# Layer 0 of a four-layer convolution kernel laid out by row block and group, with sampling weights built along the free axis

## The chip, the cores and the metric

The kernel runs on one core of one Trainium2 chip. The metric is the device time of one execution in microseconds (us). Before the change three runs gave a median of 5566.41 us (5564.74 to 5567.42). The engines are named as in the profile: PE (matmul, with its weight loads PEld), DVE, ACT, POOL, and SP, which here only issues transfers.

## What is computed

An input x of shape (8, 128, 96, 96), float32, goes through four layers. Each adds to x a function of its normalised value (32 groups of 4 channels). Layer 0 is a deformable convolution; the change rewrites it:

```python
x = x + _L0_conv_ref(_gn(x), dw_w, dw_b, gn_w, gn_b, om_w, om_b)   # deformable, 8 groups x 9 taps
x = x + conv3x3(_gn(x), L1_kernel)                                 # dense, 128 -> 128
x = x + layer2(_gn(x))                                             # depthwise on sign(x) and on x
x = x + layer3(_gn(x))                                             # scan over rows, 9 taps

# inside layer 0
x1 = gelu(norm(depthwise3x3(x) + dw_b))            # norm over the whole image
om = einsum('nhwc,oc->nhwo', x1, om_w) + om_b      # per group: 18 offsets and 9 masks
samp = gather(y0, x0) * (1-ly)*(1-lx) + ...        # bilinear, at tap position + offset
out = sum over the 9 taps of samp * mask
```

Both kernels use that with small offsets (a flag is computed, and a slow branch with a table in DRAM is there for the rest) every sampled point lies within two rows and columns of its pixel. Bilinear sampling then is a sum over 25 shifts (sy, sx), -2 to 2 each, of a weight times the shifted image. The weight of a shift is a sum over taps of a product of two "tents" max(0, 1 - |offset - distance|), one in y and one in x, the first times the mask.

## The kernel before

**The planner.** In layers 0 to 2 work is written as tasks (`Plan.task`): engine, price, function, dependences, due time, buffers. When the kernel is built, `Plan.order` (from line 165) runs through time with these prices, starts on each free engine the ready task that is due first and for which buffers are free, and so gives each engine a fixed order. On the chip engines follow that order and wait on semaphores. A due time only sets this order; DMA issues on SP are tasks as well.

**Layer 0 before.** The partitions hold 64 channels of the upper and of the lower half of an image (NB = 2 halves); the other 64 channels lie in the free axis. Two padded images (`xqs`) are kept. An image is worked on in 12 bands of 2 x 4 rows, 96 bands in all, one per STEP = 25 of due time.

`image(i, at)` loads the rows (L499, L503), takes statistics on DVE (L563), normalises on ACT (L618), does the depthwise convolution in nine taps per band on PE (L654; three bands of the first image on DVE, L646 and L648), evicts (L674), squares for the statistics (L683) and stores x1 to DRAM (L691).

`chunk(i, c, at, made)` does a band: x1 is loaded (L757), gelu (L764), the offsets and masks are projected on PE (L774) into partitions that stand for (group, tap), evicted (L793), and made into three tents for y and three for x on ACT (L783, L806); L835 multiplies the y tents by the mask on DVE. POOL multiplies nine pairs of tents (L878). For each of the 25 shifts PE multiplies such a pair by a 0/1 matrix (L888), which sums over taps and spreads a group's weight over its channels, into PSUM; DVE multiplies by the shifted image (L905). The products are added in one of three ways, by a string written by hand (ADDERS): PE with an identity matrix into one bank pair (L865), POOL (L923), or DVE (L912). The residual is loaded (L847); ACT evicts the sum with its total (L932), squares it (L940), and SP stores y (L945). y_stats makes the statistics of layer 1 (L955 to L959).

**Layers 1 and 2.** `conv_chunk` loads ten rows of y (L1279), normalises (L1290), makes four combinations on POOL (L1297), multiplies on PE in 128x128 tiles (L1310) and sums on DVE (L1326, L1334, L1346). The layer-1 weights km1 are made during layer 0 (L527 to L540). Layer 2 follows in 64x64 tiles (L1423, L1430) and on DVE (L1444). Layer 3 is a scan over 96 rows (L1722).

Of the kernel before, what the change touches and what calls it, by code (L numbers as in the profile page):

```python
# [53 lines left out]
FIRST_ON_DVE = (3, 6, 9)  # L54
RES_ORDER = (1, 0, 2)


def shift_groups():

    places = list(enumerate(shift_places()))  # L60
    return [
        (ry, rx, [(n, s) for n, s in places if s[0] % NR == ry and s[1] % NR == rx])
        for ry in RES_ORDER
        for rx in RES_ORDER
    ]

ADDERS = ("PDPEPPEPEEPDEPEDEEPDEPPPD", "PEEPPDPEEPEDDPEEPEDPEPPED")  # L70
LAST_ADDERS = "EDPPEEEDPEPDPEEEDPEEDEPPE"

STEP = 25
OM_SLOT = 11.42
WT_AHEAD = 6.2
ADD_LAG = 1438957.19
DW_SLOT = 2.09
DW_PACE = 3.98  # L80
# [133 lines left out]
def kernel(  # L214
# [33 lines left out]
    NB, HC = 2, P // 2  # L248

    def half(j):  # L250
        return slice(j * HC, (j + 1) * HC)
# [43 lines left out]
    km1 = const.tile([P, 4, 3, P], F32, name="km1")  # L295
    ymv = const.tile([P, N, 2], F32, name="ymv")
    y1 = dram.tile([N, P, HW], F32, name="y1")
# [117 lines left out]
    places = shift_places()  # L415
    groups = shift_groups()
    HB = H // NB
    XR, XW = HB + 2 * RS, W + 2 * RS
    NST = HB // RB
    GR = GK // NB  # L420
    flag = const.tile([1, 1], I32, name="flag")
    with ExitStack() as ph:
# [3 lines left out]
        x1d = dram.tile([N, P, HW], F32, name="x1d")  # L426


        sel = wp.tile([P, len(places), HC], F32, name="sel")
        omq = wp.tile([P, NB, 3, P], F32, name="omq")  # L430
        omb = wp.tile([P, 3], F32, name="omb")
        shift = wp.tile([P, 2 * NR], F32, name="shift")
        for t in (sel, omq, omb, shift):
            nc.vector.memset(t[:], 0.0)
# [3 lines left out]
        gnbq = wp.tile([P, NB], F32, name="gnbq")  # L438
        for j in range(NB):
            rows = slice(j * HC, j * HC + GR)  # L440
            taps = slice(j * GR, (j + 1) * GR)
# [5 lines left out]
            put_off(shift[rows, :], c_shift[taps, :])  # L447
            put_off(omb[rows, :], om_b[:, taps].rearrange("k r -> r k"))
            for b in range(NB):
                for m in range(NB):  # L450
                    put_off(
                        omq[half(b), j, :, m * HC : m * HC + GR],
                        om_wT[half(j), :].rearrange("c (k r) -> c k r", k=3)[:, :, m * GR : (m + 1) * GR],
                    )
            put_off(sel[rows, :, :], c_sel[taps, :, half(j)])
# [4 lines left out]
        xqs = [wp.tile([P, XR, NB, XW], F32, name=f"xq{i}") for i in range(2)]  # L460

        def zero_edges(xq):
            nc.gpsimd.memset(xq[:, :RS, :, :], 0.0)
            nc.gpsimd.memset(xq[:, XR - RS :, :, :], 0.0)
            nc.gpsimd.memset(xq[:, RS : XR - RS, :, :RS], 0.0)
            nc.gpsimd.memset(xq[:, RS : XR - RS, :, RS + W :], 0.0)

        zero_edges(xqs[0])

        stage = xqs[1][:].rearrange("p r j w -> p (r j w)")[:, : NB * XR * W].rearrange("p (j r w) -> p j r w", j=NB, w=W)  # L470
        nmx = wp.tile([P, N], F32, name="nmx")
        ysum = wp.tile([P, N, 2, NST], F32, name="ysum")
        yd = wp.tile([P, N, 2], F32, name="yd")
        beyond = wp.tile([P, 2 * N * NST], F32, name="beyond")
        nc.vector.memset(beyond[:], 0.0)

        plan = Plan()
        for name, n, psum in (
# [4 lines left out]
            if psum:  # L483
                tiles = [pp.tile([P, CB, 512], F32, name=f"ps_{name}{k}") for k in range(n)]
            else:
                tiles = [wp.tile([P, NB, FB], F32, name=f"{name}_{k}") for k in range(n)]
# [1324 lines left out]
```

## Time and profile before

| what | us |
|---|---|
| median of three runs | 5566.41 |
| profiled execution, its span | 5563.9 |
| PE busy | 5382.1 (97%) |
| weight loads busy | 3019.0 (54%) |
| DVE busy | 4838.8 (87%) |
| ACT busy | 3375.6 (61%) |
| POOL busy | 4552.9 (82%) |
| first product of layer 0 starts (L905) | 121.3 |
| last matmul of layer 0 ends (L865) | 3439.8 |
| first matmul of layer 1 starts (L1310) | 3455.3 |
| layer 3 begins, about | 4800 |

The core's mean granted PE clock was 0.992. It moved 360.67 MB in 413,202 DMA packets; SP's queue had 386,080 of these. A group of the profile names the source line, engine, operation, output and inputs, shape and count, then busy time, mean ns of one, idle time of the engine just before, and what ended it. Busy time is a union: operations of one engine overlap at their ends, and records of matmuls overlap far more, so a mean duration is not a pitch. For a pitch the starts of successive instructions are compared in the timeline.

### The profile page before, as it was taken

To read this page: it belongs to the slowest core of one execution; us is meant where nothing else is said; L and a number is where in the kernel's file an instruction comes from. 1 tells how busy PE (TensorE), PEld (TensorE's weight loads), DVE (VectorE), ACT (ScalarE), POOL (GpSimd) and SP (SyncE) were. 2 spreads that over 40 slices of the span, in tenths; PEclk is the share of its full clock that TensorE was granted. 3 is DMA by queue.
4 is the path that set the end of the run, shared out by engine and by line. 5 is a ranking of instruction groups with operands and counts; after the bars stand their busy time and mean duration, and the time that the engine had idled before them with its cause. 6 is when DMAs were issued, how large, how long until landed. Compare 5 with 4: busy or idle time off the path is not lost. (4 is left out here: it accounts for less than half of the span.)

```text
span 5563.9 us, 128984 instructions
## 1 busy us (share of the span) xinstructions
PE 5382.1 (97%) x53121; PEld 3019.0 (54%) x53121; DVE 4838.8 (87%) x6858; ACT 3375.6 (61%) x4820; POOL 4552.9 (82%) x2834
## 2 busy tenths in 40 slices
PE   6999999999999999999999998999999999999999
PEld 3554454454454454454454444545455554699999
DVE  6889889889889889888888997699999998688887
ACT  5666756656756756656766663477787777533333
POOL 1999999999999999999999998699999998522222
PEclk9999999999999999999999999999999999999999
DMA  5122112122121221211111111222222222223232
GB/s 135 55 61 58 56 58 60 54 60 58 56 59 58 57 61 58 57 60 57 49 49 47 38 43 38 59 68 68 67 65 68 66 65 51 83 103 103 100 106 80
DMA packets 413202, 360.67 MB, mean 65 GB/s; under 512 B 239072, under 2 KB 410608, under 8 KB 412608
## 3 DMA queue, kind: packets, MB, share of 16 engines
q1 hardware_dynamic: 386080, 312.91, 20.0%
q10 hardware_dynamic: 26160, 37.86, 1.9%
q8 instruction: 423, 6.93, 0.5%
q0 software_dynamic: 368, 1.57, 0.1%
q14 instruction: 171, 1.40, 0.1%
HBM read 201.26 MB, written 150.99 MB: 63 GB/s over the span
## 5 line engine op out<-in xcount | busy, mean ns | idle before, releaser
L888 PE MATMUL ps_w<-wt,sel 64*64 64x384 f32 x19200 | 1856.5, 488 | 48.3 <-DVE h L835 15.1
L905 DVE TENSOR_TENSOR pr<-ps_w,xq 128x768 f32<-128x768 f32 x1824 | 1672.4, 950 | 203.0 <-PE ps_w L888 153.0
L878 POOL TENSOR_TENSOR wt<-h,h 128x768 f32<-128x768 f32 x864 | 1581.7, 1835 | 191.6 <-PE ps_w L888 112.5
L923 POOL TENSOR_TENSOR acc<-acc,pr 128x768 f32<-128x768 f32 x882 | 1615.6, 1833 | 64.3 <-DVE pr L905 49.9
L888 PEld LDWEIGHTS ps_w<-wt,sel 64*64 64x64 f32 x19200 | 748.0, 133 | 906.3 <-issue 279.7
L1310 PE MATMUL pv_C<-dC,km 128*128 128x384 f32 x2304 | 777.3, 492 | 11.2 <-POOL dC L1297 4.8
L865 PE MATMUL ps_s<-pr,idq 64*64 64x384 f32 x7536 | 759.5, 484 | 1.8 <-DVE pr L905 1.3
L1444 DVE SCALAR_TENSOR_TENSOR ps_C<-xqC,w2s,ps_C 128x768 f32<-128x768 f32 x674 | 684.9, 1016 | 84.2 <-ACT ps_C L1482 69.7
L793 ACT ACTIVATE o<-ps_w,omb 128x768 f32<-128x768 f32 x192 | 172.5, 898 | 807.3 <-PE ps_w L774 702.2
L1661 POOL TENSOR_TENSOR xtD<-xtD,cr 128x384 f32<-128x384 f32 x192 | 192.3, 1002 | 572.1 <-ACT cr L1660 509.8
L654 PE MATMUL ps_w<-xq,dwd 64*64 64x384 f32 x6696 | 635.5, 485 | 8.3 <-DVE h L835 3.4
L1310 PEld LDWEIGHTS pv_C<-dC,km 128*128 128x128 f32 x2304 | 426.6, 190 | 359.0 <-issue 49.6
L905 DVE TENSOR_TENSOR ps_w<-ps_w,xq 128x768 f32<-128x768 f32 x480 | 460.4, 959 | 97.2 <-PE ps_w L888 96.2
L783 ACT ACTIVATE h<-o,shift 128x768 f32<-128x768 f32 x576 | 533.1, 926 | 11.7 <-ACT o L793 0.8
L806 ACT ACTIVATE h<-h 128x768 f32<-128x768 f32 x576 | 485.9, 844 | 17.4
L1461 POOL TENSOR_TENSOR ptC<-ptC,ptC 128x768 f32<-128x768 f32 x255 | 472.8, 1854 | 1.1
L865 PEld LDWEIGHTS ps_s<-pr,idq 64*64 64x64 f32 x7536 | 309.4, 133 | 299.6 <-issue 159.2
L912 DVE TENSOR_TENSOR acc<-ps_w,acc 128x768 f32<-128x768 f32 x480 | 456.8, 952 | 6.8
L774 PE MATMUL ps_w<-x1c,omq 64*64 64x384 f32 x4608 | 436.3, 493 | 21.8 <-DVE pr L905 18.0
L654 PEld LDWEIGHTS ps_w<-xq,dwd 64*64 64x64 f32 x6696 | 284.4, 133 | 271.0 <-issue 119.7
L1722 PE MATMUL ps_b<-tr,km 128*128 128x192 f32 x2304 | 407.2, 325 | 2.8 <-DVE tr L1707 2.8
L1722 PE MATMUL ps_a<-tr,km 128*128 128x192 f32 x2304 | 405.5, 324 | 0.0
(201 smaller groups left out, 7162.3 us busy)
## 6 DMA issues: line engine op xcount, KB each, us to landing
ywC<-y SPq DMA_DIRECT2D x80, 480.0 KB, 3.9
acc<-in_x SPq DMA_DIRECT2D x192, 192.0 KB, 3.3
x1c<-x1d SPq DMA_DIRECT2D x192, 192.0 KB, 3.3
y<-y SPq DMA_DIRECT2D x96, 384.0 KB, 3.0
x<-oC SPq DMA_DIRECT2D x192, 192.0 KB, 2.8
out<-xtD ACTq DMA_DIRECT2D x24, 1536.0 KB, 5.7
x1d<-x SPq DMA_DIRECT2D x93, 384.0 KB, 2.8
xtD<-x SPq DMA_DIRECT2D x23, 1536.0 KB, 6.9
```

The costliest lines, as they stand in the source:

```text
L654: nc.tensor.matmul(ps.tile[half(j), b, :FB], dwd[half(b), j, t, :], xq[half(b), r0 : r0 + RB, j, c0 : c0 + W], start=(t == 0), stop=(t == ...
L783: nc.scalar.activation(h, o, AF.Abs, bias=shift[:, k * NR + r : k * NR + r + 1])
L806: lambda h=h: nc.scalar.activation(h.tile[:], h.tile[:], AF.Relu, bias=1.0, scale=-1.0),
L865: nc.tensor.matmul(total.tile[half(j), b, :FB], idq[half(b), :], pr.tile[half(b), j, :], start=first, stop=last)
L878: lambda wt=wt, hy=hy, hx=hx: nc.gpsimd.tensor_tensor(wt.tile[:], hy.tile[:], hx.tile[:], ALU.mult),
L888: nc.tensor.matmul(ps.tile[half(b), j, :FB], sel[half(j), n, :], wt.tile[half(j), b, :], start=True, stop=True)
L905: nc.vector.tensor_tensor(view(pr.tile), view(ps.tile), x_s, ALU.mult)
L923: lambda pr=pr, acc2=acc2: nc.gpsimd.tensor_tensor(acc2.tile[:], acc2.tile[:], pr.tile[:], ALU.add),
L1310: nc.tensor.matmul(flat(ps), km1[:, k, x_, :], d.tile[:, k, :, x_ : x_ + W], start=(x_ == 0), stop=(x_ == 2))
L1444: nc.vector.scalar_tensor_tensor(view, rows8(src, t), w[:, t : t + 1], view, ALU.mult, ALU.add)
L1461: lambda a=parts[0], b=pt: nc.gpsimd.tensor_tensor(a.tile[:], a.tile[:], b.tile[:], ALU.add),
L1722: nc.tensor.matmul(ps[:, at_f : at_f + nf], km[:, k, t, :], tr[:, par, :, v : v + HW2], start=(t == 0), stop=(t == NT - 1),)
```

## The change

The planner is kept. Layer 0 is written anew; layers 1 to 3 keep their work, apart from where layer 1 gets its weights and how it reads y.

- **Layout.** A chunk is one row out of every six: `BR = H // 16` = 6 chunks per image, 48 in all. Partitions are (row block y of 16, group g of 8); the free axis is (16 channels of the group, 96 columns). One padded image `xq` is kept in place of two, for the depthwise convolution.
- **Padded rows through DRAM.** After normalisation `copy_rows` stores the image, in padded rows of 100, to `xnd`; the shifted rows come back in the new layout, ten loads `xs` per image, five in use at a time. Border rows of zeros for `xnd` are stored at the start from ACT's queue.
- **Projection.** PE projects 2 x 108 rows of om for 1536 pixels in four tasks; ACT evicts, SP stores to `omd` and loads it back with (row block, group) in the partitions and taps in the free axis.
- **Weights.** ACT makes three tents for all taps in four passes and a fifth for the flag. POOL (DVE for the first chunk) makes the 25 weights of each (row block, group, column) in 18 operations along the free axis, with stride-zero operands; ACT copies them to PSUM, five shifts at a time.
- **Products.** DVE multiplies 128x1536: the weight is read from PSUM with stride zero over the 16 channels.
- **Sums.** PE adds each product with an identity in 16 tiles of 32x32 (row tile r to bank r, channel quarter f to output partitions 32 f). The residual is one more such add, by the standard deviation, of the middle row, so x is not loaded again; x's mean is added in layer 1's coefficients. No adds are left on DVE and POOL, and no selection by PE.
- **y** is stored by (row in block, row block, channel) in four transfers per chunk; layer 1 loads its ten rows in pieces that end at block borders. Its weights are loaded and made at the beginning of layer 1 (the same six operations). The branch with the table follows the new layout of y.

The diff's core:

```diff
-FIRST_ON_DVE = (3, 6, 9)
-RES_ORDER = (1, 0, 2)
...
-ADDERS = ("PDPEPPEPEEPDEPEDEEPDEPPPD", "PEEPPDPEEPEDDPEEPEDPEPPED")
-STEP = 25
+FIRST_ON_DVE = (2, 5, 8, 11)
+CH, SHIFT, PE_KEEP = 46.0, 9.0, 4.0
+LOAD_AT, NORM_AT, CONV_AT, CONV_STEP, CONV_PACE = -90, -45, -35, 18, 1.6
+OM_STEP, SLOT_AT, COPY_AT = 2.5, 25, -5
...
-    y1 = dram.tile([N, P, HW], F32, name="y1")
+    y1 = dram.tile([N, BR, YB, P, W], F32, name="y1")
...
+        omd = dram.tile([N * BR, YB, NG * GR, W], F32, name="omd")
+        xnd = dram.tile([N, BR, YB + 1, P, XW], F32, name="xnd")
...
+        for i in range(N):
+            for d, y in ((0, 0), (RS, YB)):
+                nc.scalar.dma_start(
+                    xnd[i, d : d + RS, y].rearrange("d c w -> c d w"), zero.rearrange("p (d w) -> p d w", w=XW)
+                )
...
+            ("s", 1, [P, NQ, 512], True, True), ("wb", 2, [P, 512], True, True), ("w", 1, [P, CB, 512], True, False),
+            ("xs", 5, [P, GC, XW], False, True), ("pr", 3, [P, GC, W], False, True), ("y", 1, [P, NQ, FB], False, True),
+            ("om", 1, [P, 3, K2, W], False, True), ("tt", 1, [P, 2, 3, K2, W], False, True),
+            ("wx", 2, [P, 3, 3, NS, W], False, True), ("x1", 2, [P, NB, FB], False, True),
+            ("x1c", 1, [P, YB, W], False, True), ("oe", 2, [P, YB, W], False, True),
...
+            def copy_rows(d):
+                r, up = (d - RS) % BR, int(d < RS)
+                for b in range(NB):
+                    for j in range(NB):
+                        nc.sync.dma_start(
+                            xnd[i, d, b * YB // NB + up : (b + 1) * YB // NB + up, half(j), :].rearrange("y c w -> c y w"),
+                            xq[half(b), RP + r : RP + HB : BR, j, :],
+                        )
...
+                        xnd[i, j % BR, j // BR : j // BR + YB].rearrange("y (g c) w -> (y g) (c w)", g=NG),
...
+                        omd[n, :, m * HM : (m + 1) * HM].rearrange("y r w -> r y w"), oe.tile[:HM]
...
+                    omd[n].rearrange("y (g k) w -> (y g) (k w)", g=NG),
...
+                (lambda: nc.scalar.activation(own(1), offs(), AF.Abs), [tt, om]),
+                (lambda: nc.scalar.activation(own(1), own(1), AF.Identity, bias=1.0, scale=-1.0), [tt]),
+                (lambda: nc.scalar.activation(own(0), offs(), AF.Relu, scale=-1.0), [tt, om]),
+                (lambda: nc.scalar.activation(own(2), offs(), AF.Relu), [tt, om]),
...
+                lambda: nc.scalar.activation(offs(), own(1), AF.Relu, scale=-1.0, accum_out=beyond[:, n : n + 1]),
...
+            on = nc.vector if n == 0 else nc.gpsimd
...
+                lambda: on.tensor_tensor(
+                    wx.tile[:, :, :, 1 : NS - 1].rearrange("p d y x w -> p d y (x w)"),
+                    tripled(rows(tx(1))),
+                    all_ty().rearrange("p d y x w -> p d y (x w)"),
+                    ALU.mult,
+                ),
...
+            def add_all(weights, of, first, last):
+                for r in range(NQ):
+                    for f in range(NF):
+                        rows32 = slice(32 * r, 32 * r + 32)
+                        nc.tensor.matmul(
+                            total.tile[32 * f : 32 * f + 32, r, :FB], weights(rows32, f), of(rows32, f), start=first, stop=last
+                        )
...
-                        nc.vector.tensor_tensor(view(pr.tile), view(ps.tile), x_s, ALU.mult)
+                        nc.vector.tensor_tensor(
+                            pr.tile[:],
+                            wb.tile[:, sx * W : (sx + 1) * W].unsqueeze(1).to_broadcast([P, GC, W]),
+                            slot.tile[:, :, sx : sx + W],
+                            ALU.mult,
+                        )
...
+                    to = y1[i, dy].rearrange("y p w -> (y p) w").rearrange("(r l f c) w -> f l r (c w)", r=NQ, l=32, f=NF)
+                    nc.sync.dma_start(to[f], y.tile[32 * f : 32 * f + 32])
...
+        def conv_weights(at):
...
+            ld = plan.task("SP", 0.6, lambda: nc.sync.dma_start(k3s[:], k1), [], at - 100, lag=4.0)
...
-                    y1[i, :, lo * W : hi * W].rearrange("p (r w) -> p r w", w=W),
...
+                r = lo
+                while r < hi:
+                    z = min(hi, (r // BR + 1) * BR)
+                    nc.sync.dma_start(
+                        yw.tile[:, top + r - lo : top + z - lo, 1 : W + 1],
+                        y1[i, r % BR : r % BR + z - r, r // BR].rearrange("d p w -> p d w"),
+                    )
+                    r = z
```

## The prediction

> **What bounds the kernel now.** I read the stages first (busy time by stretch), then the costliest groups, then single instructions in order of time for the true pitch of each operation. Stretches show us busy and, in brackets, instructions for PE, weight loads, DVE, ACT and POOL; then clock, DMA share and GB/s.
>
> ```profile
> 0.00:121.00 121.00, 69.49 (x740) 35.70 (x740) 76.96 (x182) 59.12 (x102) 4.54 (x14) 0.94 0.63 152
> 300.00:3100.00 2800.00, 2723.99 (x32808) 1320.70 (x32799) 2488.35 (x3000) 1765.49 (x2594) 2633.20 (x1471) 0.99 0.19 56
> 3100.00:3437.00 337.00, 335.41 (x4050) 147.57 (x4049) 332.04 (x378) 191.95 (x268) 323.27 (x181) 1.00 0.12 36
> 3437.00:3455.00 18.00, 4.15 (x32) 2.37 (x24) 2.86 (x17) 5.63 (x9) 4.53 (x23) 0.64 0.44 106
> 3455.00:4800.00 1345.00, 1324.31 (x8828) 671.57 (x8828) 1153.69 (x1758) 971.05 (x1090) 1226.62 (x863) 1.00 0.25 64
> ```
>
> Layer 0 is the first 3455 us of 5563.9: a 121 us start, 3316 us for 96 bands (414 us per image), an 18 us end. Layers 1-2 take 1345, layer 3 764; the change scarcely touches these.
>
> ```profile
> L888 PE MATMUL ps_w<-wt,sel 64*64 64x384 f32 x19200 | 1856.5, 488 | 48.3 <-DVE h L835 15.1
> L905 DVE TENSOR_TENSOR pr<-ps_w,xq 128x768 f32<-128x768 f32 x1824 | 1672.4, 950 | 203.0 <-PE ps_w L888 153.0
> L878 POOL TENSOR_TENSOR wt<-h,h 128x768 f32<-128x768 f32 x864 | 1581.7, 1835 | 191.6 <-PE ps_w L888 112.5
> L923 POOL TENSOR_TENSOR acc<-acc,pr 128x768 f32<-128x768 f32 x882 | 1615.6, 1833 | 64.3 <-DVE pr L905 49.9
> ```
>
> DVE and POOL idle mostly for PE's L888, and PE waits for almost nothing. The mean durations overlap, so I price by start to start:
>
> ```profile
> 3421.94 0.96 DVE L905 TENSOR_TENSOR ps_w<-ps_w,xq 128x768 f32<-128x768 f32 x1
> 3422.81 0.95 DVE L905 TENSOR_TENSOR pr<-ps_w,xq 128x768 f32<-128x768 f32 x1
> 3423.67 0.95 DVE L912 TENSOR_TENSOR acc<-ps_w,acc 128x768 f32<-128x768 f32 x1
> ```
>
> 768 elements cost DVE 0.87. L1346 (384) starts 0.47 before its successor, so each further 384 adds 0.40.
>
> ```profile
> 4005.01 0.82 PE L1423 MATMUL ps_C<-xqC,dgx 64*64 64x384 f32 x8
> 4005.76 8.03 PE L1310 MATMUL pv_C<-dC,km 128*128 128x384 f32 x24
> 4013.71 0.88 PE L1423 MATMUL ps_C<-vn,dgv 64*64 64x384 f32 x8
> ```
>
> A float32 matmul is two records; 24 follow each other in 8 us, 0.322 a round. In 64x64 tiles a round is four records starting some 7 ns apart, so eight cost 0.645. Changing between tile sizes adds 0.11 (last start to next start 0.41, against 0.30 between lines of one size).
>
> One image of before: PE 300 selects, 142 adds, 105 taps at 0.645 and 36 projections at 1.29: 399 of 414 us, 96%. POOL 218 x 1.77 = 386. DVE 360 x 0.87 + 36 x 0.93 + 24 x 0.47 + about 9 of small ones = 366. **PE bounds layer 0, POOL close behind.**
>
> **What the Trainium skill says.** "TensorE: Matmul & The Clock Gate", Part 3 (packing small matmuls): 16 tiles of 32x32 run together, measured at 660 ns as its span model gives, starts about 4 ns apart. The trace shows only four tiles of 64x64 doing this, 7 ns apart. "TensorEngine Tiling (Array Packing)", Key Properties: changing the mode drains the array; the trace's 0.11 agrees. "SBUF — State Buffer", Who interferes with whom: a DVE instruction with at most one SBUF input does not contend with GpSimd. L905 has one and keeps 0.87 beside a 94% busy POOL; the new product has one too. "DMA: Bandwidth & Descriptors", Specifications: below 512 B a transfer does read-modify-write. The trace's 384 B packets are nearly all reads from DRAM (mean 26 ns), its stores have 1536 B (78 ns), so no row shows small stores.
>
> **The change, part by part.**
>
> *Products.* 2400 of 768 elements become 1200 of 1536, at 0.87 + 0.80 = 1.67. The stride-zero operand in PSUM is not new: L1334 reads such a one.
>
> ```profile
> L1346 DVE TENSOR_TENSOR vn<-vn,pv_C 128x384 f32<-128x384 f32 x192 | 104.2, 549 | 14.3 <-PE pv_C L1310 14.3
> L1334 DVE TENSOR_TENSOR vn<-vn,pv_C 128x768 f32<-128x768 f32 x96 | 91.3, 951 | 25.6 <-PE pv_C L1310 25.2
> ```
>
> It takes 951, like L905's plain 950. So 150 x 1.67 = 250 per image. The 480 adds of L912 and 288 mask products of L835 leave DVE (85 per image). With bn_stats 11 and about 40 small ones of 0.2: **DVE 270 per image.**
>
> *PE.* All selections go. In their place are 26 adds per six-row chunk, each 16 tiles of 32x32. Unknown price: not below 0.645 (the stream is as long); not above 2.58 (four tiles at a time). Tiles alone argue for 0.645; sixteen starts of 7 ns (0.11) fit under a 0.322 round. I take 0.7. Projections 24 x 1.29 = 31, taps 108 x 0.645 = 70. In the instruction order PE changes tile size 880 times, 110 per image: 12. Sum 113 + 156 x 0.7 = 222; it ties with DVE only at 1.0.
>
> *POOL.* Its adds go; it builds the weights of 47 chunks, 18 operations of 15,744 elements together:
>
> ```profile
> L1297 POOL TENSOR_TENSOR dC<-ywC 128x392 f32<-128x392 f32 x384 | 357.7, 980 | 57.1 <-PE pv_C L1310 37.2 <-ACT ywC L1290 17.9 <-PE pv_C L1254 2.0
> L1400 POOL TENSOR_TENSOR sgC<-sgC,thC 128x960 f32<-128x960 f32 (+1 forms) x96 | 213.8, 2227 | 52.4 <-ACT thC L1395 52.3
> ```
>
> (2227 - 980) / 568 = 2.2 ns an element and 0.12 each: 37 us, against a DVE chunk of 45. There is one tt buffer: ACT's five 1728-element passes (8 us at L783's rate) must follow POOL's last read of it, of which the final 6 us of POOL work hide most. So about 40 per chunk. Stride-zero on POOL is not shown; below 37 has no reason, and it matters only above 45.
>
> *ACT.* About 26 us of a 45 us chunk: hidden, unless a weight copy to PSUM queues behind the 8 us of passes; I put that into the idle share below.
>
> *DMA and SP.* Per image: 12,300 small packets of x, 12,300 of x1 back, 20,700 of om out and 12,300 of padded rows out: 57,600 x 26 ns / 16 = 94 us. Then 25.6 MB in larger ones at 1536 B per 78 ns on 16 engines: 81. Together 175 of 280; if small stores cost double, 229. SP issues about 142 transfers x 0.6 = 85. Both fit.
>
> *Next image.* In PE's order its last tap stands at add 21 of chunk 3, so 2.2 chunks, 99 us, remain. What follows: coefficients 7, load 5, gelu 3, projection 10, om out 6 and back 6, passes 8, weights 37 = 82. It fits with 17 us to spare.
>
> *Start.* First product at 121.3 before. Added: weights of the first chunk on DVE (15,744 x 1.04 ns + 18 x 0.2 = 20), om through DRAM 12, behind five row loads 7, border zeros on ACT's queue (4,096 packets x 26 / 16 = 7), longer passes 5; less 6 for fewer coefficient steps and no selection: first product at 166.
>
> *End.* Last product to first layer-1 matmul: 18.6 before. A doubled eviction 0.7, three more stores 1.8, y loads in up to three pieces and the sum over places 2: 23. The layer-1 weights (six operations, 3 us) lie beside y's way through DRAM. The split y loads (1280 packets, 2 us more of landing) are hidden by three buffers and PE's 8 us per chunk. The branch with the table is not taken: nothing.
>
> *Sum.* 8 x 270 less 11 (first statistics lie in the start) = 2149 of DVE. The bounding engine reached 96% before; the same gives 2239. So 166 + 2239 + 23 = 2428 in place of 3455: -1027. With 3 for a slower first y load the span is 5563.9 - 1027 + 3 = 4540. The median of the runs stands 2.5 above the span: **4542 us.** At 99% and a start of 150 it is 4460, at 93% and 180 it is 4630.
>
> **Rivals.** (1) *Weights come late*: small stores cost double, the chain of 82 passes 99, DVE idles at each image's start. Against it: the spare 17; for it: one om, one tt, one projection buffer in PSUM. With 25 us per image: 4740. (2) *PE becomes the bound*: four streams from the same partitions run at half rate, 1.29 per add: (113 + 201) / 0.96 = 327 per image in place of 281: 4910. For it: the trace shows at most two streams. (3) *Slower than before*: the four column tiles of a row group take turns, 2.58 per add: 515 / 0.96 = 536 per image, about 6580. This decides from where an image takes (3455 - 166 - 23) / 8 = 408: add price (408 x 0.96 - 113) / 156 = 1.79. The two column tiles of L888 share a row group and don't take turns, which speaks against it. (4) Nothing gained, because the removed work was hidden: PE's 96% excludes most of that.
>
> **Numbers.** Forecast 0.74 (its own range 4450 to 4640), (1) 0.12, (2) 0.10, (3) 0.03, (4) 0.01. Range 4450 to 4740, which reaches into (1). About 0.2% (11 us) is what a measurement can tell. Faster 0.96, same 0.01, slower 0.03.
>
> **What would show it.** Products at 1536 elements starting 1.67 apart and DVE about 96% busy between 166 and 2405; adds near 0.7 start to start, PE near 80%; POOL near 85%. If PE is full and DVE waits for it, (2) holds; if DVE's gaps stand at every sixth chunk and end on POOL or DMA, (1). Wrong would be a product pitch above 1.8, or layers 1-2 longer by over 20 us.

## The result, and the profile after

The changed kernel takes **95,733.7 us** (median of four runs, 95,729.0 to 95,740.2), the kernel before 5565.84: 17.20 times as long, 95% interval 17.18 to 17.23. The prediction was 4542.

First the stretches of the changed kernel: us busy and, in brackets, instructions for PE, weight loads, DVE, ACT and POOL; then clock, DMA share and GB/s.

```profile
217.00:2793.00 2576.00, 2061.63 (x46675) 806.88 (x46671) 2161.04 (x1599) 1192.06 (x1570) 1722.10 (x845) 0.92 0.52 139
2793.00:93550.00 90757.00, 2595.64 (x6630) 1236.25 (x6598) 14075.08 (x21556) 294.38 (x327) 50211.88 (x55310) 0.51 0.11 19
93550.00:94843.00 1293.00, 1220.52 (x7436) 625.71 (x7436) 1148.76 (x1658) 868.31 (x968) 1128.34 (x818) 0.97 0.24 61
94843.00:95738.00 895.00, 870.83 (x6009) 806.05 (x6008) 713.64 (x1476) 365.01 (x701) 293.77 (x247) 0.99 0.28 93
```

The reader is to see that layer 0 in its new form is over at 2793, from the first product at 217 to the last, and that 90,757 us follow which are in no stretch of the kernel before. The costliest groups of the page say what runs there:

```profile
L1180 POOL DMA_INDIRECT gt<-table,idx x55296 | 50211.2, 908 | 40158.7 <-DVE wq L1176 22932.4
...
L1194 DVE TENSOR_REDUCE sm<-gt 96x128 f32<-96x4608 f32 x768 | 6011.9, 7828 | 26.5
...
L989 DVE TENSOR_TENSOR pr<-ps_wb,xs 128x1536 f32<-128x1536 f32 x1200 | 2016.3, 1746 | 396.9 <-PE ps_s L955 299.7
L955 PE MATMUL ps_s<-pr,idr 32*32 32x384 f32 x38400 | 1198.8, 517 | 239.2 <-DVE pr L989 231.8
```

L1180 and L1194 stand inside the branch with the table (L1084 to L1219). It works out layer 0 a second time, for offsets of any size: POOL issues 72 gathers for each of 768 rows, 55,296 in all, at 0.91 us each. The gathers keep POOL busy for 50,211 us of the branch; for 40,159 POOL idles before them, 22,932 of these waiting for DVE's L1176. The flag was set, so nearly all of the difference is a branch that the prediction took as not taken. (This branch reads the bias of the offsets anew, L1103, and so does not have the first of the faults below.) Three questions follow. Why is the flag set? What would the change have taken without that? And where is that off the prediction?

The products and sums are as foreseen. In the last image, which has no next image beside it, the timeline shows:

```profile
2759.15 33.36 DVE L989 TENSOR_TENSOR pr<-ps_wb,xs 128x1536 f32<-128x1536 f32 x20
...
2760.95 0.94 PE L955 MATMUL ps_s<-pr,idr 32*32 32x384 f32 x32 [0.73 <-DVE pr L989]
2762.61 0.94 PE L955 MATMUL ps_s<-pr,idr 32*32 32x384 f32 x32 [0.72 <-DVE pr L989]
```

Twenty products take 33.36 us, 1.67 each; PE waits 0.72 or 0.73 for each of them. In the trace 813 pairs of adds have no other matmul between them. Most of these adds wait for a product; the 350 that start less than 0.8 us after the one before start 0.67 after it (median), and none follows closer.

### The profile page after: what moved, and what is told of

The parts are those of the page before. It is cut to its first block, busy times and chain, and to the rows that moved or that the text cites. A ratio compares the mean times of both kernels' runs of the same rounds, so it can differ in the third digit from the quotient of the medians.

```text
span 95738.4 us, 299514 instructions
## 1 busy us (share of the span) xinstructions
PE 6846.6 (7%) x67518; PEld 3518.2 (4%) x67518; DVE 18194.9 (19%) x26516; ACT 2809.0 (3%) x3700; POOL 53364.9 (56%) x57227
## 5 line engine op out<-in xcount | busy, mean ns | idle before, releaser
L1180 POOL DMA_INDIRECT gt<-table,idx x55296 | 50211.2, 908 | 40158.7 <-DVE wq L1176 22932.4
L1187 DVE TENSOR_TENSOR gt<-gt,wq 96x4608 f32<-96x4608 f32 x768 | 3804.7, 4954 | 67801.5 <-DMA gt<-table,idx 67801.5
L1194 DVE TENSOR_REDUCE sm<-gt 96x128 f32<-96x4608 f32 x768 | 6011.9, 7828 | 26.5
L989 DVE TENSOR_TENSOR pr<-ps_wb,xs 128x1536 f32<-128x1536 f32 x1200 | 2016.3, 1746 | 396.9 <-PE ps_s L955 299.7
L955 PE MATMUL ps_s<-pr,idr 32*32 32x384 f32 x38400 | 1198.8, 517 | 239.2 <-DVE pr L989 231.8
L359 PE MATMUL ps_dw<-xn_g,dwd_g 128*128 128x384 f32 x3456 | 1139.7, 491 | 25.1 <-ACT xn_g L351 25.1
L1142 PE MATMUL om<-omw,xr 128*96 128x216 f32 x1536 | 772.2, 606 | 4263.4 <-DMA xr<-x1d 4250.3
L1177 DVE TENSOR_TENSOR wq<-wq,loc 96x72 f32<-96x72 f32 x3072 | 756.3, 288 | 0.0
L899 POOL TENSOR_TENSOR tt<-tt,om 128x2592 f32<-128x2592 f32 x47 | 267.5, 5692 | 851.1 <-ACT om L875 436.2
L359 PEld LDWEIGHTS ps_dw<-xn_g,dwd_g 128*128 128x128 f32 x3456 | 657.0, 190 | 503.6 <-ACT xn_g L351 25.8
L692 PE MATMUL ps_w<-xq,dwd 64*64 64x384 f32 x6336 | 593.2, 509 | 109.1 <-ACT x L721 100.5
L1791 POOL TENSOR_TENSOR xtD<-xtD,cr 128x384 f32<-128x384 f32 x192 | 192.1, 1001 | 573.0 <-ACT cr L1790 511.0
L955 PEld LDWEIGHTS ps_s<-pr,idr 32*32 32x32 f32 x38400 | 447.8, 106 | 925.8 <-DVE pr L989 618.7
```

The costliest lines, as they stand in the source:

```text
L359: nc.tensor.matmul(ps[:, b, :FB], dwd[:, t, :], xn[:, r0 : r0 + RB, c0 : c0 + W], start=(t == 0), stop=(t == K2 - 1),)
L692: nc.tensor.matmul(ps.tile[half(j), b, :FB], dwd[half(b), j, t, :], xq[half(b), r0 : r0 + RB, j, c0 : c0 + W], start=(t == 0), stop=(t == ...
L955: nc.tensor.matmul(total.tile[32 * f : 32 * f + 32, r, :FB], weights(rows32, f), of(rows32, f), start=first, stop=last)
L989: nc.vector.tensor_tensor(pr.tile[:], wb.tile[:, sx * W : (sx + 1) * W].unsqueeze(1).to_broadcast([P, GC, W]), slot.tile[:, :, sx : sx + W ...
L1142: nc.tensor.matmul(om[:W, 0, : 3 * GK], xr[:], omw[:], start=True, stop=True)
L1177: nc.vector.tensor_tensor(wq[:, :, q], wq[:, :, q], loc[:, 2, :], ALU.mult)
```

## Why the flag is set: two faults

These lines of the changed kernel matter and are not in the diff's core:

```python
        junk = wp.tile([P, NB, FB], F32, name="junk")                                  # L426
        bias_in, bias_by_g = (junk[0:1, j, : 3 * GK] for j in range(2))                # L427
...
                    bias_by_g.rearrange(...), bias_in.rearrange(...)                   # L517, DVE
                        b.tile[:HM, 0, m : m + 1], bias_by_g[:, ...], one[:], ...      # L540, PE
...
                        junk[:], x1.tile[:], AF.Square, bias=ndwb[:], accum_out=...    # L728, ACT
```

**Fault 1.** The bias of the offsets passes through the tile `junk`, into which L728 throws the squares of every band. The planner is not told that L540 must come first. The timeline of the changed kernel near the start:

```profile
53.60 0.25 DVE L517 COPY junk<-junk 1x216 f32<-1x216 f32 x1
61.60 0.92 ACT L728 ACTIVATE junk<-x,ndwb 128x768 f32<-128x768 f32 x1
...
66.08 0.51 PE L540 MATMUL ps_w<-one,junk 1*108 1x1 f32 x4 [0.88 <-DVE LyT L535]
```

PE reads at 66.08 as bias what ACT has written at 61.60: squares of a band. All offsets and masks get a wrong constant.

**Fault 2.** The check of the offsets (L875) reads 1 - |offset| from the tile `tt`, and the first weight operation (L899) multiplies the y tents in the same tile by the mask, in place. L899 depends on the tents alone (`chain = [tents]`), so the planner may put it first. The timeline of the second chunk:

```profile
207.66 1.63 ACT L868 ACTIVATE tt<-om 128x1728 f32<-128x1728 f32 x1
...
209.36 5.67 POOL L899 TENSOR_TENSOR tt<-tt,om 128x2592 f32<-128x2592 f32 x1 [207.54 <-ACT tt L868]
...
215.06 1.64 ACT L875 ACTIVATE om<-tt 128x1728 f32<-128x1728 f32 x1 [3.84 <-POOL tt L899]
```

The check starts when L899 has ended. In 17 of the 48 chunks of the trace it comes behind L899 like this, and a tent times a negative mask counts as an offset beyond 1. In those chunks ACT, which follows its planned order, also waits for POOL, 3.8 to 7.8 us each time and 93 together. (The expectations below have 18 chunks, 5.65 us and 102.)

I saw fault 2 first and took it for the whole cause (theory A, with theory B as its rival: another cause). Four runs tested this.

**e1: the check first.**

```diff
-            chain = [tents]
+            chain = [checks[-1:]]
```

> One dependence is added: the first weight operation of a chunk (L899) waits for that chunk's check of the offsets (L875). Theory A (18 of the 48 checks read the y tents after L899 has multiplied them by the mask, so the flag is set although no offset passes 1): the branch is not taken. The changed kernel's span less the branch (2799 to 93549 us) is 4988; the 18 waits of ACT for L899 (5.65 us each, 102 together) go too, of which some reaches the end: 4880 to 4990 us. Theory B (the flag is set for another reason: an offset really passes 1, or the column sums hold something else): about 95,700 us, as before the edit. The prediction on record would have 4542.

Measured: 95,536.0 us (95,527 to 95,540), ratio 17.18 (17.16 to 17.20). All 48 checks stood ahead of L899, and the branch was taken. Theory A as the only cause falls.

**e2: the flag times 0.**

```diff
-            nc.vector.tensor_scalar(flag[:], m2[:], 0.0, None, ALU.is_gt)
+            nc.vector.tensor_scalar(flag[:], m2[:], 0.0, None, ALU.mult)
```

> The order of the changed kernel is kept as it is, misplaced checks included; only the last step of the flag multiplies by 0 in place of comparing with 0, so the offsets no longer decide on the branch (that decision is left out). Theory A and theory B alike: the branch alone is the 90,000 us, so 4940 to 5000 us. If part of the time lay elsewhere (a slow path of layers 1 to 3, or waits in front of the branch), more than 5100. Against e1 it gives the price of the 18 waits of ACT alone: 0 if they are hidden, up to 102 us.

Measured: 4985.75 us (4973.4 to 4987.4), ratio 0.897 (0.895 to 0.898). The branch is the whole of the 90,000 us, and nothing else of that size is hidden in front of or behind it. This run leaves the decision out and keeps both faults, the wrong bias included, so it serves for timing alone.

**e3: the x half of the check alone.**

```diff
-                lambda: nc.scalar.activation(offs(), own(1), AF.Relu, scale=-1.0, accum_out=beyond[:, n : n + 1]),
+                lambda: nc.scalar.activation(
+                    om.tile[:, 0].rearrange("p k w -> p (k w)"), tt.tile[:, 0, 1].rearrange("p k w -> p (k w)"),
+                    AF.Relu, scale=-1.0, accum_out=beyond[:, n : n + 1],
+                ),
```

> The check reads and clears only the x half of the tents (864 of 1728 elements), which L899 does not overwrite; the planner's order stays. Left out: the check of the y offsets. Theory A: the flag stays 0 with no change of order, 4880 to 5000 us. Theory B with an offset that really passes 1 in x, or with columns of the sums that hold something else: 95,700 us.

Measured: 95,557.0 us (95,553 to 95,722), ratio 17.18 (17.16 to 17.21). The x tents are never overwritten, and they set the flag. So the offsets themselves are too large (theory B), which led to the bias in `junk`.

**e4: the kernel before, its branch always taken.**

```diff
-            nc.vector.tensor_scalar(flag[:], m2[:], 0.0, None, ALU.is_gt)
+            nc.vector.tensor_scalar(flag[:], m2[:], 0.0, None, ALU.is_ge)
```

> The kernel before, with its flag compared by 'greater or equal' to 0, so that its branch is always taken. If the branch costs the same in both kernels: 5566 + 90,750 = 96,300 us, within 1%. If the branch is slow only behind the new layer 0 (its new layout of the result, its new row blocks), the time would be off that by thousands of us.

Measured: 95,869.2 us, ratio 17.24 (17.21 to 17.27); 90,307 more than the kernel before. The branch costs much the same in both kernels: its price is not one of the new layout.

Theory C then says that either fault alone sets the flag. Two more runs complete the square.

**e5: both dependences.**

```diff
-                    [ev], when + 18, uses=[x1],
+                    [ev, *maps], when + 18, uses=[x1],
...
-            chain = [tents]
+            chain = [checks[-1:]]
```

> Two dependences are added: the squares of the bands (L728), which use the tile 'junk' as a place to throw results, wait until the bias of the offsets, which lies in the same tile from 53.60 us on, has been read by PE (L540 at 66.05 us; the first square is at 61.60); and the first weight operation waits for the check, as in e1. Theory C (the overwritten bias makes offsets that pass 1, and either fault alone sets the flag): the branch is not taken, and with e2 at 4985.75 us less part of the 102 us of ACT's waits for L899, 4920 to 4985 us. Theory B' (the flag has still another cause): about 95,550 us. The prediction on record has 4542; what is left above it would then be layer 0 and layer 1 themselves.

**e6: the first of them alone.**

> Only the first of e5's two dependences: the bias is kept, the 18 misplaced checks stay. Theory C: 18 checks still read tents times mask, some of which are negative, so the branch is taken: 95,500 to 95,750 us. If the overwritten bias was the only cause: 4920 to 4990 us.

| bias kept | check first | us | |
|---|---|---|---|
| no | no | 95,733.7 | the change as it is |
| no | yes | 95,536.0 | e1 |
| yes | no | 95,770.6 | e6 |
| yes | yes | **4917.0** (4907.2 to 4923.1) | e5 |

e6's ratio is 17.22 (17.19 to 17.26), e5's 0.884 (0.883 to 0.886). Theory C is shown: each fault suffices, and mending one alone brings nothing. e5 is 69 us below e2. It differs from it in the order that both dependences give; the 17 waits of ACT for L899 are gone in it, and DVE's idle time from the first to the last product falls from 393 to 336 us. The runs with the branch tell the two dependences apart, since the branch comes behind the products. From the first to the end of the last product the change takes 2575 us, e6 (bias kept) 2571, e1 (check first) 2505 and e5 2496. So nearly all of it comes from the place of the check. In e3, which keeps the planned order but whose check has nothing to wait for in L899, and is half as long, the stretch is 2524. About half of the 93 us of waits thus reached the end.

## What the change takes without the branch

e5's profiled execution has a span of 4909.6, where the prediction's sum has 4540. By the prediction's own stages:

| stage | predicted | e5 | off |
|---|---|---|---|
| first product at | 166 | 208.8 | +43 |
| first to end of last product | 2239 | 2496.4 | +257 |
| to the first matmul of layer 1 | 23 | 19.1 | -4 |
| the rest | 2112 | 2185.3 | +73 |

**The +73.** Layers 1 and 2 do what they did, in PE's groups and in POOL's. By lines, one thing is new: `mean += xmean` (L1385), by which x's mean comes back in. It has one element per partition. The timeline of e5, with POOL's line before and its last line in that time:

```profile
2882.98 1.83 POOL L1590 TENSOR_TENSOR ptC<-ptC,ptC 128x768 f32<-128x768 f32 x1
2884.43 17.55 DVE L1385 TENSOR_TENSOR mean_yC<-mean_yC,xmean 128x1 f32<-128x1 f32 x1
...
2900.16 1.80 POOL L1590 TENSOR_TENSOR ptC<-ptC,ptC 128x768 f32<-128x768 f32 x1
2903.57 0.98 PE L1438 MATMUL pv_C<-dC,km 128*128 128x384 f32 x1 [16.53 <-DVE vn L1455]
```

POOL runs eleven more instructions in these 17.55 us, each beginning as the last ends. L1385 ends at 2901.98, when POOL's unbroken work does (2901.96), and PE stands 16.53 us behind it. Both inputs of L1385 lie in SBUF. The Trainium skill, "SBUF — State Buffer", Who interferes with whom, says that such a DVE instruction contends with a GpSimd instruction that reads SBUF. The trace agrees, with a price that the size of the instruction doesn't show: 0.16 us for the first two, before POOL's work on layer 1 begins, and 7.8 to 17.6 for the six others, 70 together.

**e7: the same sum with one input in SBUF.**

```diff
-                    nc.vector.tensor_tensor(mean[:], mean[:], xmean[:, i : i + 1], ALU.add)
+                    nc.vector.tensor_scalar(mean[:], mean[:], xmean[:, i : i + 1], None, ALU.add)
```

> e5 with one edit more, in layer 1: mean += xmean (L1385, 128x1, both inputs in SBUF) becomes a tensor_scalar with xmean as the scalar operand, one input in SBUF. In e2 the six of them that run beside a busy POOL took 3.7 to 17.6 us, 66.4 together, the two beside an idle POOL 0.16, and layers 1-2 took 68 us longer than before the change. Theory D (DVE waits for POOL because of the two SBUF inputs, and PE for DVE): e5 less 60 to 68 us. Rival (the time is charged to that instruction but belongs to the split loads of y or the longer issue on SP): within 10 us of e5.

Measured: **4837.7 us** (4836.5 to 4847.9), ratio 0.871 (0.869 to 0.872), 79 below e5, somewhat more than the 60 to 68 expected. All eight now take the same, by the answer for that line:

```profile
L1385 DVE TENSOR_SCALAR mean_yC<-mean_yC,xmean x8: 214/214/215, 2720.5 to 3747.2; 128x1 f32<-128x1 f32 x8
```

From the first layer-1 matmul to the end e7 takes 2110.2, the prediction's 2112. Theory D is shown; the split loads of y cost nothing that can be seen, as predicted.

**The +257.** DVE idles 341 us between the first and the last product of e7 (here and below the sum of its gaps over 0.15 us). One such gap, with the lines before it (start, us, engine):

```profile
1643.65 1.53 PE L692 MATMUL ps_w<-xq,dwd 64*64 64x384 f32 x16
1644.01 0.35 SPq L852 DMA_DIRECT2D om<-omd  x1
...
1650.37 1.64 ACT L865 ACTIVATE tt<-om 128x1728 f32<-128x1728 f32 x1 [7.34 <-DMA om<-omd]
...
1656.66 0.88 ACT L721 ACTIVATE x<-ps_w,dwb 128x768 f32<-128x768 f32 x1
...
1657.69 5.40 PE L692 MATMUL ps_w<-xq,dwd 64*64 64x384 f32 x32 [7.82 <-ACT x L721]
...
1663.02 2.88 PE L955 MATMUL ps_s<-pr,idr 32*32 32x384 f32 x96
1664.25 3.42 DVE L989 TENSOR_TENSOR pr<-ps_wb,xs 128x1536 f32<-128x1536 f32 x2 [9.92 <-PE ps_s L955]
```

This is to be read from below. DVE waits 9.92 for a product buffer, which an add (L955) has to free. The add stands in PE's queue behind taps (L692). These waited 7.82 for the one buffer `w` that taps and projections share, until ACT evicts it (L721). The band had been ready to evict since 1645.2; but in ACT's queue the eviction stands behind the four passes of tents, and ACT sits idle at the first of them, until the offsets issued at 1644.01 have come back from DRAM. No engine is full: from the first to the last product of the change, e5 and e7 PE is busy 80 to 82%, DVE 84 to 86%.

Which part of that chain decides? Theory E: the blocks of taps. Theory F: the 8 us of tents, by their length or by their rank in ACT's queue. All the following start from e7.

**e8: no keeping of a tile size.**

```diff
-CH, SHIFT, PE_KEEP = 46.0, 9.0, 4.0
+CH, SHIFT, PE_KEEP = 46.0, 9.0, 0.0
```

> e7 with PE_KEEP 0 in place of 4, so that the planner no longer keeps TensorE on one tile size for up to 4 us: the nine taps of a band (6.1 us of PE in one piece in e2) are mixed with the adds. Theory E (DVE's 58 us of idle time per image come from adds that queue behind blocks of taps, with three product buffers of 1.66 us each between): e7 less 60 to 150 us. Rival F (they come from ACT: evictions of taps and projections queue behind the 8 us of tents, and PE's one projection buffer with them): within 25 us of e7, or slower by the added changes of tile size (0.11 each).

Measured: 4958.2 us (4950.6 to 4963.6), ratio 0.891 (0.890 to 0.893): 120 slower than e7. PE changes tile size 1090 times in place of 856, which at 0.11 is 26 us and not on DVE; DVE's idle time grows to 429 us. Taps were mixed in, and the gaps got longer. Theory E in the form of this edit falls.

**e9: tents in halves.** Each of the five passes becomes two by axis, of about 0.9 us, and L899 waits for all ten.

```diff
+            for q, a in enumerate((1, 0)):
...
+                    t = plan.task("ACT", 0.92, fn, prev, at - 66 + 1.0 * len(tents), uses=uses)
```

> e7 with the four passes of tents and the check cut into two halves by axis (ten pieces of about 0.9 us in place of five of 1.64), y first, due 1 us apart; the weight operations wait for all ten. In image 4 of e7 DVE idles 20.6 us in three gaps (9.9, 4.3, 6.3 us) in which ACT runs the 8 us of tents while an eviction or a copy of weights waits behind them. Theory F (the length of the pieces holds the evictions up): 20 to 140 us less than e7 (4838). If the planner still puts the pieces side by side, or theory F is wrong: within 20 us of e7.

Measured: 4907.0 us (4904.8 to 4909.3), ratio 0.882 (0.881 to 0.884): 69 slower than e7. The planner put the pieces side by side, as the expectation allowed, but the loss was not expected.

**e11: two taps of nine** (and the flag times 0).

```diff
-                for t in range(K2):
+                for t in (0, K2 - 1):
```

> e7 with two of nine taps per band (the other seven are left out, and the flag is multiplied by 0 so that other offsets can't set it): the blocks of nine taps, 6.1 us of PE, shrink to 1.4. In image 4 of e7 the gaps of DVE that end on an add behind such a block sum to about 20 of 320 us. Theory E in its narrow form (blocks longer than the three product buffers cover): images 1 to 6 get shorter by about 20 us each, some 120 us, and the start by 10 to 40. If all of DVE's idle time hangs on the taps (the single projection buffer that taps and projections share): by 40 us each, 280 us. If on neither: under 40 us in all, from the start.

Measured: 4724.3 us (two runs, 4720.2 and 4728.5), ratio 0.850 (0.848 to 0.851), 113 below e7; DVE idles 211 us. That is the size of the narrow theory E. But the taps also hold `w` for a shorter time, and in this run ACT never waits for the offsets, so it doesn't tell E from what follows.

**e12: e9, and evictions and copies due earlier; e13: these dues alone, on e7.**

```diff
-                ev = plan.task("ACT", 1.08, evict, prev, when + 16, uses=[ps, x1])
+                ev = plan.task("ACT", 1.08, evict, prev, when - 100, uses=[ps, x1])
...
-                        [t], when + 2, uses=[ps, oe],
+                        [t], when - 100, uses=[ps, oe],
...
-                    chain[-1], at + SHIFT * (sy - 1), uses=[wb, wx], lag=0.1,
+                    chain[-1], at + SHIFT * (sy - 1) - 100, uses=[wb, wx], lag=0.1,
```

> e9, and ACT's evictions of taps and projections and its copies of weights are due 100 us earlier for the planner, so that ACT takes them ahead of a tent as soon as they can run. Theory F: the three gaps of each of seven images go (20.6 each, 144 us), and the first copy of weights no longer waits behind the second chunk's tents (16 us at the start): 4838 - 100 to 4838 - 170, so 4670 to 4740 us. Theory E alone: within 30 us of 4838.

> e7 with the earlier dues of e12 alone, the passes of tents whole (1.64 us each). Theory F with the order as the cause, not the length: nearly all of e12's gain, 4680 to 4770 us. With the length as the cause: near e9, and above e12 by over 50 us.

Measured: e12 4774.6 us (4768.0 to 4791.2), ratio 0.858 (0.857 to 0.860), 63 below e7; e13 4866.9 (4861.3 to 4873.8), ratio 0.875 (0.873 to 0.877), 29 above it. Neither length nor rank explains this alone. In e12 ACT still stands idle for the offsets for 168 us. The planner fixes ACT's order with an estimate of when they land: 4 us for the store, 5 for the load back. In e7 5.0 to 8.8 us pass in 31 of 48 chunks from the second store's issue to the load's, more in the others, and 5.3 to 7.7 from that to L865 in the 25 chunks where ACT waited for it. An eviction due first is still put behind a pass that, by the estimate, will have run before it. That is theory G, and it can be tested by estimates alone: no operation is added or removed.

**e14: e12 with longer estimates; e15: e7 with them; e16 and e17: e12 and e7 with longer ones still; e18: e16, but not for the first chunk.** The lines below have e14's numbers; the table has those of the others.

```diff
-            t = plan.task("DVE", 0.8, aggr1, stats1, when)
+            t = plan.task("DVE", 3.9, aggr1, stats1, when)
...
-                outs, at - 100, uses=[x1], lag=5.0,
+                outs, at - 100, uses=[x1], lag=8.0,
...
-                kept.append(plan.task("SP", 0.6, keep, evs, at - 85 + OM_STEP * 2 * m, uses=[oe], lag=4.0))
+                kept.append(plan.task("SP", 0.6, keep, evs, at - 85 + OM_STEP * 2 * m, uses=[oe], lag=7.0))
...
-                kept, at - 75, uses=[om], lag=5.0,
+                kept, at - 75, uses=[om], lag=9.0,
```

> e12 with other estimates for the planner: the landing of the offsets' store 7 us (4), of their load back 9 us (5), of x1's load 8 us (5), and the sums of statistics on DVE 3.9 us (0.8; L764 alone takes 3.1). Nothing is added or taken away, only the order differs. Theory G (in e12 ACT stands idle 168 us in 23 waits for the offsets' load at the head of its queue, with evictions behind, because the order expects it earlier): those waits shrink by more than half and the time falls by 40 to 120 us, to 4650 to 4735. Rival (the gaps come from the one projection buffer that taps and projections share, whatever the order): within 25 us of e12 (4774.55).

> e7 with the estimates of e14 and none of e12's edits. Theory G: ACT's waits for the offsets (144 us, 18 times in e7) shrink and the time falls by 40 to 120 us, to 4720 to 4800. Rival: within 25 us of 4837.67. Slower by over 25 us would say that the order on this machine can't be foreseen by these estimates at all.

> e14 with still longer estimates (store 10, load back 14, x1's load 12 us), longer than what e7's trace shows in most chunks (5.3 to 10). Theory G: no better than e14 by over 20 us, since what lands in time needs no later order; ACT's waits for the offsets nearly gone. Rival as in e14.

> e7 with e16's estimates (store 10, load back 14, x1's load 12 us; statistics 3.9) and none of e12's edits. If the estimates alone carry the gain (theory G in full): within 40 us of e16, 4640 to 4720. If pieces and dues are needed too, so that evictions get past the tents: 4730 to 4800, near e15 (4751). PE's waits for evictions (92 us for taps in e7, 3 in e16) should fall in the first case and stay in the second.

> e16 with the old estimates (4, 5, 5 us) for the first chunk alone. If the later first product is the price of the long estimates at the start: first product near 205 us in place of 236.8 and 15 to 32 us less than e16 (4681.26), 4650 to 4666. If the order of the rest hangs on that (it is planned anew behind it): anything within 60 us of e16.

| run | estimates (store, load back, x1's load) | us | ratio (interval) | DVE idle | ACT for the offsets | PE for evictions |
|---|---|---|---|---|---|---|
| e7 | 4, 5, 5 | 4837.7 | 0.871 (0.869 to 0.872) | 341 | 144 | 98 |
| e15 | 7, 9, 8 | 4751.3 | 0.854 (0.853 to 0.855) | 240 | 176 | 27 |
| e17 | 10, 14, 12 | 4688.2 | 0.843 (0.842 to 0.844) | 175 | 63 | 6 |
| e12 | 4, 5, 5 | 4774.6 | 0.858 (0.857 to 0.860) | 270 | 168 | 100 |
| e14 | 7, 9, 8 | 4751.7 | 0.854 (0.853 to 0.856) | 201 | 108 | 48 |
| e16 | 10, 14, 12 | 4681.3 | 0.842 (0.840 to 0.843) | 153 | 36 | 13 |
| e18 | e16's from chunk 1 | 4681.7 | 0.842 (0.841 to 0.843) | 165 | 32 | 14 |

DVE's idle time is that between first and last product. The two right columns are us waited from 500 to 2400, from the list of waits: L865 (L868 in the split form) for its load, and matmuls of taps and projections (L692, L829) for ACT. For e7 and then e17 that list has:

```profile
ACT tt L865 <- DMA om<-omd: 143.9, 18, 10.5
...
PE ps_w L692 <- ACT x L721: 43.2, 7, 8.0
PE ps_w L829 <- ACT oe L837: 39.7, 5, 9.0
```

```profile
ACT tt L865 <- DMA om<-omd: 62.7, 21, 9.0
...
PE ps_w L829 <- ACT oe L837: 3.1, 3, 2.1
...
PE ps_w L692 <- ACT x L721: 1.8, 1, 1.8
```

From e7 to e17 only four numbers told to the planner differ, and the time falls by 150 us. From e15 to e17 and from e14 to e16 the price of the statistics stays and the three landings alone grow: 63 and 70 us. Theory G is shown in this form: the planned order, which rests on short estimates, puts evictions that PE needs behind a waiting ACT, and an order from longer ones doesn't. Three of my expectations were wrong. e14 fell by only 23 us, which by itself is what the rival expected, and ACT's waits fell from 168 to 108, not by half. Its trace shows one reason: DVE's idle time fell by 69, but DVE's small operations between first and last product (all but the products and the bn_stats) took 145 us in place of e12's 116. L624, a tensor_scalar of 128x32 with 24 calls, took 52.5 in place of 26.1; its long calls, up to 5.79, all end 0.04 after a POOL instruction does. In e15 ACT's own waits were to shrink: they grew to 176 us, and the time still fell by 86, while PE's waits for evictions fell from 98 to 27. It is not how long ACT waits that counts, but what stands behind it. And e16 was to bring no more than 20 us over e14; it brought 70. Its estimates are longer than the trip that e7's trace shows, so a margin helps beyond the true value; why, and which of the four numbers does most, was not tried apart. e12's pieces and dues are not needed: e16 and e17 lie 7 us apart with overlapping runs (4676.7 to 4689.6, 4686.1 to 4698.9).

e18 answers for the start: with the old estimates for the first chunk its first product comes at 209.6 in place of 236.8, as expected, but the time is the same (4681.7, 4674.3 to 4684.7). The later order gave the 27 us back: image 0 takes 310 us in place of 273.

e16 to e18 are the fastest versions here, each faster than the kernel before by 15.7 or 15.8%.

## Why the prediction was wrong, point by point

**The step that failed** is this one: "The branch with the table is not taken: nothing." It was carried over from the kernel before, where the flag stays 0, as if the flag were a property of the data. It is a value that the new code computes, with a new check, from newly computed offsets. The page of the kernel before does not show the branch, but the code gives its count: 768 rows of 72 gathers. At the 0.91 us that each took these alone are 50,000 us, and the whole branch took 90,757. A condition with such a price deserved a rival with a chance. And both faults could be read: which tile each operation writes and who reads it before, set against the order in which the planner puts them. The order of ACT against POOL and PE was at hand, and I read it for waits, not for what a tile holds when it is read.

**What the sum said of the rest**, against e7, where both faults and L1385 are mended:

- *Products*: 1.67 predicted, 1.66 to 1.67 measured. Right. So is the claim that a product with its weight in PSUM keeps this beside a busy POOL.
- *Adds*: 0.7 chosen between 0.645 and 2.58; 0.67 measured. The Trainium skill has sixteen tiles of 32x32 run together ("TensorE: Matmul & The Clock Gate", Part 3), and here they do. That its 660 ns lie near 0.67 us says less: its table names neither float32 nor 384 columns. Rivals (2) and (3) hung on this and are refuted.
- *Changes of tile size*: 880 predicted, 856 in e7, from last start to next start 0.41 as before.
- *POOL*: 37 us per chunk predicted; chunk 18 of e7 takes 1132.45 to 1170.22, 37.8. Of chunks 18 to 35 all but three take that; 21, 27 and 33 take 49.7. In chunks 18 to 35 the weights are ready 14 to 39 us ahead of the first product, so rival (1), weights too late, isn't what holds DVE either.
- *DVE's own work*: 2149 us predicted; busy 2153 in e7 and 2157 in e17 between first and last product. Right.
- *Idle share*: "The bounding engine reached 96% before; the same gives 2239." This is the second step that failed. DVE's share is 2153 / 2499 = 86% in e7 and 2157 / 2337 = 92% in e17. The 96% was PE's, which before fed the others and waited for almost nothing. It was carried over to an engine with other dependences: DVE here depends on PE's and ACT's fixed orders, and those on a trip through DRAM. The stretches, e7's first and then e17's:

```profile
208.00:2707.00 2499.00, 2052.40 (x46627) 801.72 (x46627) 2153.23 (x1599) 1191.54 (x1570) 1730.89 (x846) 0.93 0.52 143
```

```profile
231.00:2568.00 2337.00, 2027.02 (x46483) 803.43 (x46483) 2157.48 (x1599) 1189.82 (x1561) 1731.87 (x846) 0.95 0.57 151
```

- *ACT*: 26 of 45 us, hidden "unless a weight copy to PSUM queues behind the 8 us of passes; I put that into the idle share". The busy time was right (1192 us in 48 chunks is 25 each), the place nearly; but evictions queue there too, and their delay passes through PE to DVE.
- *Start*: 166 predicted, 208 in e7. The weights on DVE took 19.2 us (20 predicted). The tents of chunk 0 could begin only at 164.7, some 27 later than a first product at 166 allows (20 for the weights and 8 for the passes come between). More than half of these 27 are there when the first image's statistics end: ACT's square root (L783) runs at 122.6, its counterpart before (L742) at 101.0, 22 earlier, and the sum has only 7 for that, the border zeros. From 64 to 91 SP issues 24 stores of padded rows (L653), for which the sum has no term, and meanwhile ACT waits 15.7 us (4.39 and 11.30) for stores of x1. Then the weights, ready at 192.1, wait 16 more for their copy (L978), which in ACT's queue stands behind chunk 1's tents. That is the pattern of theory G, but the longer estimates don't mend it: e17's first product comes at 231.2.
- *End*: 23 predicted, 19 measured. *Layers 1 to 3*: +3 predicted; +73 in e5, all of it L1385, and nothing in e7. More than 20 us there was one of the prediction's own signs of being wrong. I had quoted the rule on SBUF inputs for the products and not held it against the small operations that the change puts beside a busy POOL.

With the faults mended and the order planned on longer landings the kernel reaches 4681 to 4688 us, inside the range given for the change itself (4450 to 4740) and 3% above its 4542. That does not confirm the prediction: the change as made is not that kernel, and the idle share, the start and L1385 had to be found first.

## What to carry to other kernels

A branch that data decides is a term of the sum like any other: give it its full price and ask from which new values, in which tiles, its condition is computed and what may overwrite them in the order that a scheduler chooses. Where the orders of engines are fixed in advance, estimate a trip through DRAM long rather than short, as it paid here except at the start: an engine that waits at the head of its queue holds up everything behind it, and through a shared buffer the engines that seemed to have slack. Hold every new instruction, even one of one element, against what runs beside it.

## What the runs showed of the hardware that was not expected

- A DVE add of 128x1 with both inputs in SBUF took up to 17.6 us beside POOL, and 0.16 without. It ended where POOL's unbroken row of instructions did, after eleven of them: it was not let in between two. A tensor_scalar isn't free of this either: L624 (128x32) took 0.23 us at its shortest and up to 5.79 in e14, and each of its calls over 1 us ended 0.04 after a POOL instruction.
- PE's granted clock in layer 0 is 0.92 in the changed kernel and 0.95 in e17, with PE busy 80 and 87% of the stretch; before it was 0.99 at 97%. Why, and what it costs, these runs don't say.
- A gather by POOL's indirect DMA keeps POOL busy for 0.91 us (0.903 to 1.112), and there are 55,296 of them.
